# Cross attention, first quarter: each unit's key/value work begins with the chunk that comes from DRAM

## Chip, cores and metric

The kernel is one program on one core of a Trainium2 chip. The metric is device time in microseconds (us). Before the change three runs took 3841.57, 3847.80 and 3852.76 us, a median of 3847.8 us.

## What is computed

Two decoder layers on 16 sequences of 112 rows of width 512 (float32), with a context of 375 rows for each sequence. Layer 0 is causal self attention, a block with fp8-rounded activations (self attention and cross attention, whose results are joined before one projection), and a mixture of experts; layer 1 is self attention, cross attention over the context, and a feed-forward with ternary weights. The change lies in the cross part of the fp8 block, whose mathematics is this:

```
qx  = layernorm(fp8_linear(ln_out, wqx))               # 16 heads of 128
kvx = cond @ w_kv_x.T                                  # cond: 16 x 375 x 512
kx, vx = split(kvx);  kx = layernorm(kx)               # 8 groups of 128 each
xout = softmax(qx @ kx.T / sqrt(128)) @ vx             # two heads share a group
catq = fp8(concat(core, xout) / proj_smooth);  out = catq @ wproj.T * scale
```

## The kernel before, in words

`stage_fp8_cross` (L1178) treats the 16 heads in four quarters `q` of four heads (two key/value groups), and in each quarter the 16 sequences `b`. One pair (q, b) is a **unit**, an object of `CrossUnit` (L1060); there are 64. I number the units of the first quarter 0 to 15.

A unit loads the transposed context `ct` (two buffers) and, where a tile of 128 rows begins, the rounded activations `xq`. Its steps are:

- `queries` (L1093): the projection `ps_q`, eight matmuls, only for 14 of the 16 units of a quarter (14 tiles of 128 rows cover the 16 x 112 rows), then `normed`, into `qn`.
- `keys_values(ch)` (L1102) for the chunks 0, 1 and 2 of 125 context rows: four matmuls of 128x512 in float32 into `ps_kv` (L1113), `normed` into `kn`, and a copy into `vn` (L1118). **In the first quarter chunk 2 has no matmuls here.** Its product was made in the stage before (`EarlyKeys.product`), stored in `kv_dram`, and is loaded behind the first 250 context rows of `ct` (L1077, `self.early`).
- `normed` (L1082) takes three engines: a square on ScalarE (`sq`, L1088), a sum on VectorE (`cu_v`, L1089), reciprocal square root by two instructions on GpSimd (L517, L518), and the product on VectorE (`kn` or `qn`, L1091).
- `transpose` (L1120): `qn` and `kn` through TensorE to `qt` and `kt` (ScalarE copies them out). I call the transposes of the two key groups kT0 and kT1.
- `scores(heads)` (L1134), for heads 0 and 1, then 2 and 3: the product `ps_s`, the row extreme `ex_m` (VectorE, L1056), the exponential `pr` with its row sum (ScalarE, L1057), the reciprocal `cx_s` (L1145) and the scaling of `pr` (L1148), both VectorE.
- `transpose_probs` (L1150): `pr` through TensorE into `ps_pt` (L1156), copied by ScalarE into `pt`; each of the three chunks takes four transposes, one for each head.
- `values` (L1161): `ps_av`, then `smooth_fp8` on VectorE and GpSimd (`r_y`, `r_m`, `r_t`, `r_o`); two units later `output` (L1172), the product `ps_acc` and its addition to `x` on VectorE (L931).

The loop is a pipeline over two units: at step n it projects the new unit n while it scores unit n-1. In program order that is: queries of n, chunk 0 of n, scores 0 and 1 of n-1, chunk 1 of n, scores 2 and 3 of n-1, chunk 2 of n, output of n-2, transposed probabilities and values of n-1, transposes of n.

`kn` has one buffer, so no chunk of a new unit's `kn` can be written before the keys of the unit before it have been transposed. `vn` and `ct` have two. PSUM tags: `mm` (ps_q, ps_kv) three banks, `tr` two, `sc` (ps_s, ps_av) two, `acc` one. From the third unit on, the weights of the next quarter are prepared beside the units (`Weights.step`, L596: loads `raw` and `w_kv`, `w_mean` on VectorE, `w_cross` on ScalarE and GpSimd).

The order in which each engine runs its instructions in this stage isn't that of the program. A scheduler of the framework sorts them, by program order as priority and by its own idea of when an operand is ready; it pulls work forward where it thinks an engine would stand still. Each engine then runs its list strictly in order. SyncE (SP) issues all loads of the stage from one such list.

Of the kernel before, what the change touches and what calls it, by code (L numbers as in the profile page):

```python
# [54 lines left out]
def tile_of(b):  # L55


    return None if b % 8 == 7 else b - b // 8
# [42 lines left out]
def chunks(slot, at, c, n, rows=P):  # L101
    return slot[:rows, at : at + c * n].rearrange("p (c n) -> p c n", c=c)
# [13 lines left out]
def load_pieces(k, what, src, widths):  # L116
    pieces, at = [], 0
    for n in widths:
        pieces.append(load_piece(k, what, src[:, at : at + n]))
        at += n  # L120
    return pieces


def behind(k):


    return k.tc.issue_after(k.last_load.ins)
# [38 lines left out]
class NormedRows:  # L166
# [4 lines left out]
    def __init__(self, k, wk, rows, tags=("tr",)):  # L171
        self.k, self.wk, self.rows, self.tags = k, wk, rows, tags
        self.at = [sum(n for _, _, n in rows[:i]) for i in range(len(rows) + 1)]
        self.xt = wk.tile([P, KC, self.at[-1]], F32, tag="xt", name="xt", bufs=1)
        self.mv, self.rs = row_stats(k, [r for r, _, _ in rows])
        self.xn = []
        for i in range(min(2, len(rows))):
            self.normalize(i)
# [360 lines left out]
class Weights:  # L539
# [30 lines left out]
    def keys_values(self, k, src):  # L570
        with behind(k):
            self.kv = load_piece(k, "kv", src)
        return lambda: self.center_keys(k, self.kv), None
# [486 lines left out]
class CrossUnit:  # L1060
# [3 lines left out]
    def __init__(self, k, wk, q, b, w, heads):  # L1064
        self.k, self.wk, self.q, self.b, self.w = k, wk, q, b, w
        self.heads, self.tile = heads, tile_of(b)
        if self.tile is not None:
            self.xq = wk.tile([P, KC, P], F32R, tag="xq", name="xq", bufs=2)
            k.nc.sync.dma_start(out=self.xq.bitcast(F32), in_=k.xx_dram[self.tile])
        self.ct = ct = wk.tile([P, KC * SC + 12], F32, tag="ct", name="ct", bufs=2)  # L1070
        if q == 0:
            n = SC - CC
            self.ct, self.early = chunks(ct, 0, KC, n), ct[:CC, KC * n :].rearrange(
                "p (h d) -> p h d", d=P
            )
            k.nc.sync.dma_start(out=self.ct, in_=k.a["ctx_t"][b][:, :, :n])
            k.last_load = k.nc.sync.dma_start(out=self.early, in_=k.kv_dram[b])  # L1077
        else:
            self.ct = chunks(ct, 0, KC, SC)
            k.last_load = k.nc.sync.dma_start(out=self.ct, in_=k.a["ctx_t"][b])  # L1080
# [21 lines left out]
    def keys_values(self, ch):  # L1102
        k, wk, nc = self.k, self.wk, self.k.nc
        w = chunks(self.w.kv, 0, KC, 512)
        if ch == 0:
            self.kn = wk.tile([CC, NCH, 2, P], F32, tag="kn", name="kn", bufs=1)
            self.vn = wk.tile([CC, NCH, 2, P], F32, tag="vn", name="vn", bufs=2)
        if ch == NCH - 1 and self.q == 0:
            pkv = self.early
        else:  # L1110
            pkv = k.psum.tile([CC, 4, P], F32, tag="mm", name="ps_kv", bufs=3)
            for c in range(KC):
                nc.tensor.matmul(  # L1113
                    pkv, self.ct[:, c, ch * CC : (ch + 1) * CC], w[:, c, :],
                    start=c == 0, stop=c == KC - 1,
                )
        self.normed(self.kn[:, ch], pkv[:, 0:2, :])
        nc.scalar.copy(self.vn[:, ch], pkv[:, 2:4, :])  # L1118
# [59 lines left out]
def stage_fp8_cross(k):  # L1178


    with k.stage("s2b", mm=3, tr=2, sc=2, acc=1) as wk:
        units = []
        for n in range(4 * B + 2):
            q, b = divmod(n, B)
            new = last = None
            if q < 4:
                if b == 0:
                    w, heads = k.next_w, Heads()
                new = CrossUnit(k, wk, q, b, w, heads)
                units.append(new)  # L1190
                new.queries()
                new.keys_values(0)
            if 0 < n <= 4 * B:
                last = units[n - 1]
                last.scores((0, 1))
            if new:
                new.keys_values(1)
            if last:
                last.scores((2, 3))
            if new:  # L1200
                new.keys_values(2)

            first = new is None or q == 0
            if n > 1 and first:
                units[n - 2].output()
            if last:
                last.transpose_probs()
            if n > 1 and not first:
                units[n - 2].output()
            if last:  # L1210
                last.values()
            if new:
                new.transpose()
            if b == 2 and q < 3:
                k.next_w = Weights(k, "cross", q + 1, wk, raw=2)
            if b >= 2 and q < 3:
                k.next_w.step(1)
            if b == 2 and q == 3:
                with behind(k):
                    k.weights["shared"] = load_pieces(k, "shared", k.a["shared_w"], MOE_WIDTHS)  # L1220
# [565 lines left out]
def stage_ffn(k):  # L1786
# [66 lines left out]

STAGES = (
    stage_attn0, stage_fp8_self, stage_fp8_cross, stage_moe, stage_attn1,
    stage_cross1, stage_ffn,
)
# [147 lines left out]
```

## Time and profile before

| | |
|---|---|
| median of three runs | 3847.8 us |
| profiled execution | 3842.72 us, of which the span from first to last instruction is 3841.0 us |
| granted TensorE clock, mean | 0.975 |
| TensorE busy over the span | 3627.2 us (94%) |
| VectorE, ScalarE, GpSimd busy | 1764.6, 1437.4, 926.1 us |
| first quarter of the cross stage | from about 930 to 1262 us of the span |
| costliest group | L1113, `ps_kv`, 1408 records, 638.3 us |

How to read it: all times in views of the trace are microseconds from the start of the span. A float32 matmul shows as two records. The TensorE records overlap in the trace, since their ends are modelled, so I compare starts with starts. In a timeline, a row has start, length, engine, line, operation and tiles; `[1.36 <-DVE pr L1148]` at its end says that the engine stood idle for 1.36 us before it, until VectorE's instruction of line 1148 released it.

### The profile page before, as it was taken

The page shows a single profiled execution, that of the slowest core. Times are in us where ns is not written, and L with a number is a line of the kernel's source. Part 1 is how long each engine was busy: PE and PEld are TensorE (multiplying, and loading weights), DVE is VectorE, ACT ScalarE, POOL GpSimd, SP SyncE. Part 2 cuts the span into 40 slices and gives each one's busy share as a digit, 9 for nine tenths or more (in the row PEclk, how much of TensorE's full clock was granted, in tenths as well). Part 3 has the DMA queues.
Part 4 walks back from the last instruction along what each step waited for, and adds up shares of the span by engine and source line. Part 5 has one row for each costly group of instructions (what it writes and reads, how often), then busy time and mean ns, then how long its engine had stood idle before and what let it go on. Part 6 is the DMA issues. An engine that isn't in the chain of part 4 may idle for free.

```text
span 3841.0 us, 46297 instructions
## 1 busy us (share of the span) xinstructions
PE 3627.2 (94%) x16482; PEld 2338.3 (61%) x16482; DVE 1764.6 (46%) x3872; ACT 1437.4 (37%) x4149; POOL 926.1 (24%) x1314
## 2 busy tenths in 40 slices
PE   7888898899899999999999999999989999999999
PEld 4455787787555566656666654555544445556788
DVE  4445777776544544544445543111243343214333
ACT  2455675554444444444444430111123341112222
POOL 2333555553322322222222210000132220000000
PEclk8999899999999999999999999999989999999999
DMA  2125333432211211211121113999830022222000
GB/s 78 52 101 172 113 101 120 132 128 79 76 51 52 76 52 46 71 49 52 42 84 49 44 47 121 314 320 317 298 129 12 1 71 82 72 74 81 11 12 17
DMA packets 118117, 364.56 MB, mean 95 GB/s; under 512 B 13280, under 2 KB 33248, under 8 KB 108848
## 3 DMA queue, kind: packets, MB, share of 16 engines
q1 hardware_dynamic: 105504, 332.20, 26.7%
q0 software_dynamic: 5040, 16.52, 1.2%
q10 hardware_dynamic: 7344, 12.89, 0.9%
q8 instruction: 131, 2.15, 0.2%
q14 instruction: 98, 0.80, 0.1%
HBM read 317.09 MB, written 44.47 MB: 94 GB/s over the span
## 4 chain that ended last, share of the span: by engine, by line
PE 69%; DVE 8%; POOL 5%; DMA 3%; issue 2%; ACT 2%; SPq 0%; POOLq 0%; ACTq 0%; DVEq 0%
PE ps_kv L1113 14%; PE ps L1470 5%; PE ps_av L1166 4%; PE ps_s L1141 3%; PE ps_y L1488 3%; PE ps_q L695 3%; PE ps_acc L695 3%; PE ps_u L1832 3%; PE ps_o L350 3%; PE ps_o L1814 3%; PE ps_g L1832 3%; PE ps_q L1583 3%; PE ps_p L1676 3%; PE ps_pt L1156 2%; PE ps_v L1598 1%
## 5 line engine op out<-in xcount | busy, mean ns | idle before, releaser
L1113 PE MATMUL ps_kv<-w_kv,ct 128*125 128x512 f32 x1408 | 638.3, 593 | 0.0
L1113 PEld LDWEIGHTS ps_kv<-w_kv,ct 128*125 128x125 f32 x1408 | 260.5, 188 | 276.1 <-issue 242.0
L536 POOL TENSOR_TENSOR r_o<-r_t,r_m 128x64 fp32r<-128x64 bf16 (+6 forms) x224 | 146.6, 671 | 326.6 <-DVE r_t L534 302.9
L1057 ACT ACTIVATE pr<-ps_s,ex_m 112x375 f32<-112x375 f32 (+1 forms) x272 | 157.4, 579 | 164.6 <-DVE ex_m L1056 154.1
L1089 DVE TENSOR_REDUCE cu_v<-sq 125x2 f32<-125x256 f32 (+1 forms) x248 | 118.6, 478 | 217.5 <-ACT sq L1088 217.5
L1470 PE MATMUL ps<-w_expert,xgt 128*128 128x448 f32 x560 | 216.4, 539 | 0.7 <-ACT xgt L1462 0.7
L517 POOL TENSOR_SCALAR cu_v<-cu_v 125x2 f32<-125x2 f32 (+1 forms) x248 | 48.0, 194 | 635.9 <-DVE cu_v L1089 633.6
L236 POOL TENSOR_TENSOR pr<-pr,nq_s 112x448 f32<-112x448 f32 (+1 forms) x120 | 119.4, 996 | 320.2 <-DVE nq_s L235 266.0
L518 POOL TENSOR_TENSOR cu_v<-cu_v,mhalf 125x2 f32<-125x2 f32 (+1 forms) x248 | 190.0, 766 | 20.4
L231 ACT ACTIVATE pr<-ps_s,nq_m 112x112 f32<-112x112 f32 (+1 forms) x480 | 167.2, 376 | 52.5 <-DVE nq_m L223 48.6
L1141 PE MATMUL ps_s<-kt,qt 128*112 128x375 f32 x512 | 183.5, 479 | 1.7 <-ACT pr L1057 1.3
L1056 DVE TENSOR_REDUCE ex_m<-ps_s 112x1 f32<-112x375 f32 (+1 forms) x272 | 148.2, 545 | 69.1 <-PE ps_s L1703 68.0
L1088 ACT ACTIVATE sq<-ps_kv 125x256 f32<-125x256 f32 x176 | 67.4, 383 | 272.8 <-PE ps_kv L1113 218.5
L511 ACT ACTIVATE qt<-ps_t,turned 128x448 f32<-128x448 f32 (+6 forms) x224 | 116.5, 581 | 130.4 <-PE ps_t L1125 121.8
L1166 PE MATMUL ps_av<-pt,vn 125*128 125x224 f32 x768 | 160.8, 358 | 0.0
L1470 PEld LDWEIGHTS ps<-w_expert,xgt 128*128 128x128 f32 x560 | 103.6, 190 | 92.0 <-issue 91.0
L1156 PEld LDWEIGHTS ps_pt<-ident,pr 112*125 112x125 f32 x768 | 104.5, 190 | 86.3 <-DVE pr L1148 48.8
L1141 PEld LDWEIGHTS ps_s<-kt,qt 128*112 128x112 f32 x512 | 89.9, 177 | 100.8 <-issue 59.1
L245 ACT COPY ptt<-ps_pt 112x448 f32<-112x448 f32 (+1 forms) x120 | 66.8, 565 | 223.0 <-PE ps_pt L243 223.0
L1156 PE MATMUL ps_pt<-ident,pr 112*125 112x112 f32 x768 | 119.8, 285 | 30.9 <-DVE pr L1148 29.0
L1166 PEld LDWEIGHTS ps_av<-pt,vn 125*128 125x128 f32 x768 | 143.5, 192 | 8.7 <-ACT pt L1159 4.6
L511 ACT ACTIVATE kt<-ps_t,vec 128x375 f32<-128x375 f32 (+7 forms) x240 | 131.4, 588 | 26.0 <-PE ps_t L1131 22.0
(294 smaller groups left out, 7377.4 us busy)
## 6 DMA issues: line engine op xcount, KB each, us to landing
w_expert<-in_moe_w SPq DMA_DIRECT2D x105, 896.0 KB
ct<-in_ctx_t SPq DMA_DIRECT2D x64, 750.0 KB
xq<-xq_dram SPq DMA_DIRECT2D x42, 512.0 KB
xq<-xx_dram SPq DMA_DIRECT2D x56, 256.0 KB
raw<-in_self_w SPq DMA_DIRECT2D x48, 256.0 KB
w_sum<-in_ffn_w SPq DMA_DIRECT2D x12, 1024.0 KB
cn<-in_ctx SPq DMA_DIRECT2D x16, 750.0 KB
xv<-xv_dram SPq DMA_DIRECT2D x48, 224.0 KB
```

What stands on the lines that cost most here:

```text
L231: nc.scalar.activation(pr[:, j, :], self.ps[:, j, r * t : (r + 1) * t], AF.Exp, bias=self.mx[r][:, j : j + 1], scale=-1.0, accum_out=sums[ ...
L511: k.nc.scalar.activation(dst, src, AF.Identity, bias=cols[:, 1:2], scale=cols[:, 0:1])
L518: nc.gpsimd.tensor_tensor(dst, dst, bc(k.minus_half[: dst.shape[0]], [dst.shape[0], n]), ALU.pow)
L695: k.nc.tensor.matmul(out, lhs(c), w[i][:, c, :], start=first and c == 0 and i == 0, stop=last and c == n - 1 and i == 1,)
L1056: nc.vector.tensor_reduce(mx, src, AX.X, ALU.min)
L1057: nc.scalar.activation(dst, src, AF.Exp, bias=mx, scale=-1.0, accum_out=sums)
L1113: nc.tensor.matmul(pkv, self.ct[:, c, ch * CC : (ch + 1) * CC], w[:, c, :], start=c == 0, stop=c == KC - 1,)
L1141: nc.tensor.matmul(ps, self.heads.qt[self.b][:, h, :], self.kt[:, h // 2, :], start=True, stop=True)
L1156: nc.tensor.transpose(ps[:, h, :], self.pr[:, h, ch * CC : (ch + 1) * CC], k.ident[:S, :S])
L1166: nc.tensor.matmul(av[:, 2 * g : 2 * g + 2, :], self.vn[:, ch, g, :], self.pt[:, ch, 2 * g : 2 * g + 2, :], start=ch == 0, stop=ch == NCH - 1,
L1470: nc.tensor.matmul(pp, self.xt[:, c, :], w[:, c, :], start=c == 0, stop=c == 3)
L1832: nc.tensor.matmul(pp, w[:, c, cols], xt[:, part, c, :], start=c == 0 and part == 0, stop=c == 3 and part == 1,)
```

## The change

In the first quarter a unit now does chunk 2 (the one from `kv_dram`) first, ahead of the query projection, and then chunks 0 and 1 where they stood: chunk 0 after the queries, chunk 1 between the two halves of the scores. The place after the second half of the scores, where chunk 2 stood, is empty. The tiles `kn` and `vn` are allocated by whichever chunk comes first. The other quarters keep the order 0, 1, 2. No instruction is added or removed.

```diff
@@ CrossUnit.__init__
         self.heads, self.tile = heads, tile_of(b)
+        self.kn = None
@@ CrossUnit.keys_values
-        if ch == 0:
+        if self.kn is None:
             self.kn = wk.tile([CC, NCH, 2, P], F32, tag="kn", name="kn", bufs=1)
             self.vn = wk.tile([CC, NCH, 2, P], F32, tag="vn", name="vn", bufs=2)
@@ stage_fp8_cross
                 units.append(new)
+                steps = [2, 0, 1] if q == 0 else [0, 1, 2]
+                if q == 0:
+                    new.keys_values(steps.pop(0))
                 new.queries()
-                new.keys_values(0)
+                new.keys_values(steps.pop(0))
             if 0 < n <= 4 * B:
                 last = units[n - 1]
                 last.scores((0, 1))
             if new:
-                new.keys_values(1)
+                new.keys_values(steps.pop(0))
             if last:
                 last.scores((2, 3))
-            if new:
-                new.keys_values(2)
+            if new and steps:
+                new.keys_values(steps.pop(0))
```

In the changed file, lines from 1067 on are numbered one higher, and more from the loop on.

## The prediction

> **What bounds the kernel now.** I read the busy table first. TensorE is busy for 94% of the span, so this change can win only TensorE's idle time in the stage it touches. The table by stage comes next: the stretch of the first quarter, then the second, whose units the change leaves alone.
>
> ```profile
> PE 3627.2 (94%) x16482; PEld 2338.3 (61%) x16482; DVE 1764.6 (46%) x3872; ACT 1437.4 (37%) x4149; POOL 926.1 (24%) x1314
> ```
>
> The stretches (length, then PE, PEld, DVE, ACT, POOL busy, granted clock, DMA share, GB/s):
>
> ```profile
> 930.00:1262.00 332.00, 306.95 (x1196) 192.67 (x1197) 167.25 (x416) 150.60 (x366) 92.50 (x169) 0.99 0.22 66
> 1262.00:1598.00 336.00, 331.39 (x1235) 202.56 (x1234) 164.70 (x391) 145.07 (x348) 86.48 (x159) 0.99 0.17 52
> ```
>
> TensorE lacks 25 us in the first quarter and 4.6 in the second. The view of waits for TensorE in the first quarter (total, times, longest) says for whom:
>
> ```profile
> PE ps_pt L1156 <- DVE pr L1148: 22.2, 16, 3.1
> PE ps_acc L695 <- POOL r_o L536: 1.4, 1, 1.4
> PE ps_t L1131 <- DVE kn L1091: 1.3, 2, 0.8
> ```
>
> So 22.2 us go to the transposes of the probabilities, once in a unit, waiting for VectorE's scaling of heads 2 and 3. The timeline lists them: ten of 1.36 to 1.39 (13.7), three of 0.58 to 0.90 (2.1), and 0.48, 2.85 and 3.07 in units 0 and 1. **That is the ceiling.** Why VectorE is late shows in its timeline, beside ScalarE's and TensorE's, for one of the ten:
>
> ```profile
> 1041.65 0.41 DVE L1089 TENSOR_REDUCE cu_v<-sq 125x2 f32<-125x256 f32 x1
> ...
> 1042.24 0.19 ACT L1057 ACTIVATION_READ_ACCUMULATOR pr<-ps_s,ex_m 112x1 f32 x1
> ...
> 1043.15 0.42 DVE L1091 TENSOR_TENSOR kn<-ct,cu_v 125x256 f32<-125x256 f32 x1 [1.09 <-POOL cu_v L518]
> 1043.50 0.16 DVE L1145 RECIPROCAL cx_s<-cx_s 112x2 f32<-112x2 f32 x1
> 1043.57 0.73 DVE L931 SCALAR_TENSOR_TENSOR x<-ps_acc,c_proj,x 128x512 f32<-128x512 f32 x1
> ...
> 1044.22 0.73 DVE L1148 TENSOR_SCALAR pr<-pr,cx_s 112x375 f32<-112x375 f32 x2
> ...
> 1044.68 0.47 PE L1156 MATMUL ps_pt<-ident,pr 112*125 112x112 f32 x2 [1.36 <-DVE pr L1148]
> ```
>
> The row sums are there at 1042.24 + 0.19 = 1042.43. But chunk 2's `kn<-ct` stands at the head of VectorE's list and waits for GpSimd until 1043.15, and then `x` is served first. The chain of waits runs the same way in these units: POOL L518, DVE kn, cx_s, x, pr, PE.
>
> **What moves.** I compared the built order of both programs on every engine. The scheduler doesn't put chunk 2 at the start of a unit. Its square and sum (`sq<-ct`, `cu_v`) keep their slot after the second half of the scores, but now belong to the unit one later. Its `kn<-ct` can't run there (`kn` has one buffer) and lands behind kT1, after `r_t`. So the slot before `cx_s` loses `kn<-ct`, and `x` falls behind `pr`. The scheduler also regroups TensorE: of the query projection only one matmul, not four, stands before head 2's transposes. The other four go between kT0 and kT1, where one matmul of chunk 0 stood; that one goes behind kT1. From the start of the second quarter all lists are the same.
>
> **One of the ten units, step by step**, from the second score pair (1038.67).
> - VectorE: sums at +3.76. `cx_s` follows 0.03 later and `pr` another 0.21 later, as in the first score pair of this unit (1037.68, 1037.71, 1037.92); TensorE starts 0.46 after `pr` (1044.22 to 1044.68). Head 2 is ready at +4.46 instead of +6.01, 1.55 us sooner.
> - TensorE: first four transposes at +3.11 as before, one q matmul at +3.47, ready at +3.79 (0.32 from that q to a transpose, as at 1044.92 to 1045.24). It waits 0.67 for head 2. Head 3 follows 0.33 later (the pair of `pr` takes 0.73, one 0.40), q x3 after 0.14, the last four transposes after 0.79: +5.72. Before, they began at 1046.17, or +7.50. Saved: 1.78.
> - Given back: the four q matmuls. Between kT0 and kT1 they take 1.28 (the second quarter has this order: 1258.78 to 1260.06), as long as the chunk 0 matmul that leaves (1029.75 to 1031.02, 1.27). That one, 0.86 (half of a 1.72 pair, from 2.58 for three), now lies behind kT1. Net 0.92.
> - `ps_av`: ScalarE no longer squares `ps_q` (0.60) between the copies of `pt`; 2.40 as in the unit without a projection (1066.54 to 1068.94), not 2.47. Together 0.99.
>
> Ten units: **9.9 us**. The units with waits of 0.61 and 0.58 have no query; a chunk 0 matmul (0.86) leaves the gap and `pr` comes 1.55 sooner, so both meet at about 1062.95 in the first; less 0.1 for head 3, **1.0** for both. In the one of 0.90 TensorE's order stays, the wait goes: **0.9**.
>
> **Units 0 and 1** need each queue. At the start, chunk 2's `kn` of unit 0 is made while TensorE still projects, so the wait of 0.51 before its transposes goes; the regrouped transposes give 0.6 in all. SP is more important:
>
> ```profile
> 945.50 0.55 SPq L1076 DMA_DIRECT2D ct<-in_ctx_t  x1
> 946.09 0.51 SPq L1077 DMA_DIRECT2D ct<-kv_dram  x1
> 946.65 0.33 SPq L112 DMA_DIRECT2D w_kv<-in_cross_w  x1
> ```
>
> The first waits for the buffer of unit 0's `ct`, held by `kn<-ct` (944.93 + 0.42). Then the last reader is the chunk 1 matmuls (until 941.8), so all three go 3.5 us sooner, and `w_kv` lands near 951.7, not 955.2. That matters, since VectorE's new list has three `w_mean` reductions and a `w_kv` subtraction ahead of unit 0's first `pr`. With `w_kv` at 951.7: `pr` of heads 0 and 1 at 954.4 (0.48 goes), and, adding the list's durations, `pr` of head 2 at 960.6 instead of 962.47: **1.9**. Were `w_kv` still at 955.2, the same sum ends at 963.4, a loss of 0.9; the ceiling is 3.3 + 0.6. I take 1.9, as the release is plain. Unit 1 loses a `kn<-ct` that took 1.48; `cx_s` could go 1.75 sooner, but GpSimd's `w_cross` (1.26 at 982.53) may block `pr` beside it: 0.4 to 1.74, I take **1.2**.
>
> What is costed at nothing: `sq<-ct` needs its load a unit earlier, but that is issued about 5 us sooner, when chunk 1's matmuls free the buffer, some 18 us before the square; cover gone, ScalarE would hold the exponentials. `xq` is issued about 5 us later with 11 left. `x` behind `pr` frees the one `acc` bank 18 us before it is needed. `qn` (679 to 693 ns) with its GpSimd wait now stands ahead of chunk 0's sum and `ex_m` of head 0: I get `qn` done at 1034.85, and chunk 0's square can be summed at 1035.45 (1034.59 + 0.86), so 0.6 to spare.
>
> **A rule against the change.** Row: `kn<-ct` took 424 to 1478 ns; the longest ran beside GpSimd's `w_cross`. The Trainium skill ("SBUF — State Buffer", section "Who interferes with whom") says that a VectorE instruction with two SBUF inputs and a GpSimd instruction that reads SBUF exclude each other for the whole instruction. `kn<-ct` has two such inputs, which that one row bears out, and its new place is beside `r_o` (1.17 for a unit); in the old one GpSimd had just finished. By the median row it costs 0.42; by the rule up to 1.06 more in each unit, 10.6 us over the ten if nothing covered it: gain 4. I find cover: 0.6 as above, and the 0.4 left over delays only head 0, while VectorE is done with the first `pr` pair 0.7 before chunk 1's sum. So 0 on the path, and I keep some of it for the range.
>
> **Sum.** 9.9 + 1.0 + 0.9 + 1.9 + 1.2 = 14.9 us. Against the profiled execution's 3842.7 that is 3827.8; against the median of three runs, 3847.8, it is 3832.9. The profiled execution lies among the lower of the four; I say **3832**.
>
> **Rivals.**
> - *Part of it is lost on VectorE's list* (22%): port blocking, or `pr` slowed by it, costs about 0.7 a unit, gain 7: 3840. For it: 1478 ns above, and a `pr` pair of 1.77 instead of 0.73 beside `w_cross`. Against: both in unit 1 alone.
> - *All waits vanish* (6%): gain 22, 3825. Against it: one q matmul is too little cover, 0.67 stays.
> - *Slower* (4%): `sq<-ct` stands on ScalarE ahead of head 2's exponential. If its load lands after that, heads 2 and 3 slip and TensorE has lost three q matmuls of cover. At the old delay of `pr` a unit is 0.63 longer (0.92 + 0.63 = 1.55, the break-even being 0.92 of lateness), 6.3 for ten: 3854. It decides once a load takes over 19 us. Against: the whole queue of 1.77 MB ending with `w_kv` took 9.7 us.
> - *Nothing moved* is excluded by the built orders.
>
> **Numbers.** The forecast itself has 68%. About 0.3% (11.5 us) is what a measurement tells from no change; 14.9 is close to it and medians of three scatter by 5, so faster 0.70, same 0.26, slower 0.04. Bounds: ten units at 0.6 to 1.4, unit 0 from -0.9 to 3.9, unit 1 from 0.4 to 1.74, so gains from about 7 to 22; with the scatter 3822 to 3843.
>
> **What would show it.** The wait of L1157 for `pr` falls from 22.2 to about 11.6 us (0.7 to 0.8 in the ten, 2.1 and 1.9 in units 0 and 1) with TensorE's busy time unchanged; units of 19.8 become 18.8; `w_kv` issues near 943; `kn<-ct` stands behind `r_t`, some of over 1 us. I am wrong if TensorE waits for `kt` or `ex_m` instead, if `sq<-ct` waits for a DMA, or if the ten waits stay above 1.2.

## The result, and the profile after

The changed kernel took 3834.2 us (median of 16 runs) beside 3848.1 us (16 runs of the kernel before). The ratio is **0.9964, 95% interval 0.9953 to 0.9975**: 0.36% faster, or about 14 us. The interval includes a gain of 0.25%, so "over 0.3%" is likely and not certain. The forecast was 3832, with a range of 3822 to 3843.

The profiled execution has a span of 3823.6 us, 17.4 less than before. Of that, 15.4 us lie in the first quarter. What comes before it ran 2.9 us shorter and what follows it 0.9 us longer, although the change doesn't touch either. The four lines below are from views whose lines of before were shown in the prediction: the busy table, the stretch of the first quarter (length, then PE, PEld, DVE, ACT and POOL busy, clock, DMA share, GB/s) and TensorE's waits in it.

```profile
PE 3617.8 (95%) x16482; PEld 2333.7 (61%) x16482; DVE 1770.9 (46%) x3872; ACT 1439.6 (38%) x4149; POOL 929.7 (24%) x1314
```

```profile
930.00:1245.00 315.00, 303.42 (x1193) 191.65 (x1192) 174.43 (x419) 150.79 (x364) 93.28 (x168) 0.99 0.23 70
```

```profile
PE ps_pt L1157 <- DVE pr L1149: 10.8, 14, 1.4
PE ps_t L1132 <- DVE kn L1092: 0.8, 1, 0.8
```

The two stretches don't hold quite the same work. Counted from the stage's first `ps_q` to the end of unit 15's last `ps_av`, TensorE is busy for 298.4 us (301.5 before), and about 1.7 of these 3.1 us are a spell at half clock less (last section). What shrank is the wait for `pr`: 22.2 to 10.8 us. One of the ten like units shows how. This is the timeline of all engines:

```profile
1033.19 0.19 ACT L1057 ACTIVATION_READ_ACCUMULATOR pr<-ps_s,ex_m 112x1 f32 x1
...
1033.41 0.17 DVE L1146 RECIPROCAL cx_s<-cx_s 112x2 f32<-112x2 f32 x1 [0.41 <-ACT pr L1057]
1033.61 0.74 DVE L1149 TENSOR_SCALAR pr<-pr,cx_s 112x375 f32<-112x375 f32 x2
...
1034.08 0.80 PE L1157 MATMUL ps_pt<-ident,pr 112*125 112x112 f32 x4 [0.54 <-DVE pr L1149]
1034.27 0.75 DVE L931 SCALAR_TENSOR_TENSOR x<-ps_acc,c_proj,x 128x512 f32<-128x512 f32 x1
```

Before, `kn<-ct` (with 1.09 of idle time ahead of it) and `x` stood between the row sum and `pr`. Now `cx_s` waits for ScalarE's row sum and for nothing else, and `x` comes after `pr`. TensorE waits 0.54 where it waited 1.36, and these units take 18.93 us instead of 19.81.

### The profile page after: what moved, and what is told of

The parts are those of the page before. It is cut to its first block, busy times and chain, and to the rows that moved or that the text cites. A ratio compares the mean times of both kernels' runs of the same rounds, so it can differ in the third digit from the quotient of the medians.

```text
span 3823.6 us, 46289 instructions
## 1 busy us (share of the span) xinstructions
PE 3617.8 (95%) x16482; PEld 2333.7 (61%) x16482; DVE 1770.9 (46%) x3872; ACT 1439.6 (38%) x4149; POOL 929.7 (24%) x1314
## 5 line engine op out<-in xcount | busy, mean ns | idle before, releaser
L914 DVE TENSOR_TENSOR r_y<-ps_av,r_smooth 128x448 bf16<-128x448 f32 x128 | 79.2, 619 | 126.8 <-PE ps_av L1167 122.8
```

## How the experiments are read

Whole executions scatter by several us, but the first quarter repeats to 0.3 us: a second profile of the changed kernel gave 309.75 us after 310.01. So each run is read by its first quarter, from the stage's first `ps_q` to the end of unit 15's last `ps_av`. The first four expectations count to the start of that `ps_av`, which is 2.4 us less (323.0 before, 307.6 after). "Half clock" counts the windows of 3.41 us in the quarter in which TensorE's granted clock was 0.50 (last section); each costs up to 1.7 us, half its length, and all of them lie in units 0 to 2. All numbers of the table are from the traces, except the ratio, which is to the kernel before on the same chip, with its 95% interval.

| kernel | `w_kv` issued after | wait for `pr` | half clock | units 0-2 | units 3-15 | quarter | ratio |
|---|---|---|---|---|---|---|---|
| before | 13.58 | 22.2 | 2 | 76.60 | 248.83 | 325.43 | 1 |
| changed | 10.12 | 10.8 | 1 | 70.42 | 239.59 | 310.01 | 0.9964 (0.9953-0.9975) |
| 1 before, `kn<-ct` on GpSimd | 13.71 | 10.4 | 3 | 75.18 | 239.55 | 314.73 | 0.9969 (0.9951-0.9988) |
| 2 changed, keys in place | 13.38 | 21.1 | 3 | 75.22 | 248.29 | 323.51 | 0.9999 (0.9984-1.0014) |
| 3 before, `x` later | 13.58 | 21.9 | 3 | 75.95 | 248.88 | 324.83 | 0.9992 (0.9976-1.0008) |
| 4 order 0, DRAM, 1 | 10.12 | 15.3 | 0 | 70.10 | 248.94 | 319.04 | 0.9978 (0.9969-0.9988) |
| 7 mixed order | 10.13 | 8.4 | 0 | 67.99 | 239.60 | 307.59 | 0.9948 (0.9932-0.9963) |
| 9 changed, one subtraction on VectorE | 10.12 | 8.1 | 0 | 65.59 | 239.57 | 305.16 | 0.9939 (0.9922-0.9955) |
| 10 before, the same | 13.58 | 20.4 | 1 | 72.12 | 248.83 | 320.95 | 0.9970 (0.9955-0.9986) |

In this table units 3 to 15 take one of two lengths, 239.6 or 248.3 to 248.9; runs 1 to 4 show what decides. Where TensorE's matmuls of q are regrouped (changed, 1, 4, 7, 9), 0.9 us of what units 0-2 gain is only work that moves behind `ps_av` and comes back in unit 15.

## Experiments on the steady units

Four theories of where the gain comes from: A, the place of `kn<-ct` in VectorE's list; B, earlier loads and the clock in units 0 and 1; C, that a unit begins with the chunk; D, that `x` comes after `pr`.

**1. Before, with the DRAM chunk's product on GpSimd.**

```diff
-        nc.vector.tensor_tensor(dst, src, bc(var.unsqueeze(2), [t, n, P]), ALU.mult)
+        eng = nc.gpsimd if pool else nc.vector        # pool: src is the DRAM chunk
+        eng.tensor_tensor(dst, src, bc(var.unsqueeze(2), [t, n, P]), ALU.mult)
```

> The kernel before, its order of chunks untouched; only the multiplication that normalises the DRAM chunk (kn<-ct) is given to GpSimd, so that it cannot stand in VectorE's list ahead of cx_s. Theory A (the gain is that slot: kn<-ct no longer between the scores' row sums and the normalisation of the probabilities): TensorE's wait for pr in the first quarter falls from 22.2 to 10-13 us, the quarter (first ps_q of the stage to unit 15's last ps_av) from 323.0 to 307-311 us, the total by 12-16 us to 3832-3836. Theory B (the gain comes from the earlier release of ct and so from earlier loads, and from the clock in units 0 and 1): the loads are not earlier here, so at most 3 us, quarter 320-323. Theory C (a unit must begin with the chunk): no gain, quarter 322-324.

Measured: wait 10.4, quarter 312.3 by the count of the expectation, median 3835.6. TensorE's wait for `pr` in the quarter:

```profile
PE ps_pt L1158 <- DVE pr L1150: 10.4, 13, 2.1
```

Theory A holds for the steady units: with the chunk still last, and `w_kv` no earlier, units 3 to 15 are as short as in the changed kernel (239.55 and 239.59). As in the changed kernel, `x` falls behind `pr` here; run 3 shows what that alone is worth. The quarter misses A's band by 1.3 us, and the miss lies in units 0 to 2, which gain 1.4 us where those of the changed kernel gain 6.2. Theory C falls.

**2. Changed, with the normalised keys written over the loaded ones.**

```diff
-        self.normed(self.kn[:, ch], pkv[:, 0:2, :])
+        self.normed(self.early[:, 0:2, :] if pkv is self.early else self.kn[:, ch], pkv[:, 0:2, :])
```

The transposes read them from there.

> The changed kernel, a unit still begins with the DRAM chunk, but its normalised keys are written over the loaded ones in ct, not into kn. So the multiplication waits neither for kn nor for anything of the unit before it, and the built order has it ahead of cx_s again, with the matmuls of q grouped as before (4, 1, 3). Theory A (the slot ahead of cx_s): the gain is gone though the chunk comes first; wait for pr 20-23 us, quarter 320-324, total within 3 us of before. Theory C (beginning with the chunk is what pays, whatever VectorE's list): quarter 306-311, total 12-16 us under before. Theory B (earlier loads): ct is held longer here, so no gain either, and w_kv lands as late as before or later: together with the first run it parts A from B.

Measured: wait 21.1, quarter 321.1 by that count, ratio 0.9999. VectorE's timeline in one of its units:

```profile
1043.34 0.42 DVE L1093 TENSOR_TENSOR ct<-ct,cu_v 125x256 f32<-125x256 f32 x1 [1.09 <-POOL cu_v L518]
1043.68 0.15 DVE L1148 RECIPROCAL cx_s<-cx_s 112x2 f32<-112x2 f32 x1
1043.76 0.73 DVE L931 SCALAR_TENSOR_TENSOR x<-ps_acc,c_proj,x 128x512 f32<-128x512 f32 x1
```

A unit begins with the DRAM chunk and nothing is gained. The product, `ct<-ct` here, is back ahead of `cx_s` with the same 1.09 of idle time, and `x` with it. In the changed kernel it is the single buffer of `kn` that keeps it out of this place.

**3. Before, with the output projection behind the transposed probabilities.**

```diff
-            first = new is None or q == 0
+            first = new is None
```

> The kernel before, but the output projection of the first quarter is put behind the transposes of the probabilities in the program, which takes VectorE's x additions behind pr; kn<-ct stays ahead of cx_s. Theory A (kn<-ct ahead of cx_s): most of the loss stays; wait for pr 15-21 us, quarter 315-323, total 0-8 us under before. Theory D (it is the x additions' place behind pr alone that pays): wait for pr 10-13 us, quarter 307-311, total 12-16 us under before.

Measured: wait 21.9, quarter 322.4, ratio 0.9992. The built order has `x` behind `pr`, as in the changed kernel, and such a unit takes 19.65 instead of 19.81. So `x` alone is worth about 0.16 us in such a unit; over units 3 to 15 nothing is left of it (248.88 beside 248.83). Theory D falls. The idle time ahead of `kn<-ct` is the same 1.09.

**4. Changed, in the order 0, DRAM, 1.**

```diff
-                steps = [2, 0, 1] if q == 0 else [0, 1, 2]
-                if q == 0:
-                    new.keys_values(steps.pop(0))
+                steps = [0, 2, 1] if q == 0 else [0, 1, 2]
                 new.queries()
                 new.keys_values(steps.pop(0))
+                if q == 0:
+                    new.keys_values(steps.pop(0))
```

> The changed kernel with the chunks of a first-quarter unit in the order 0, DRAM, 1 instead of DRAM, 0, 1. In the built order kn<-ct and its row sum stand after chunk 0's and before the scores' maxima; the slot ahead of cx_s is empty as in the changed kernel and TensorE's list is the same. Theory A (only that the slot ahead of cx_s is empty): as the changed kernel, wait for pr 10-12.5 us, quarter 306.5-309.5, total within 3 us of 3834. Theory C (it must be the unit's first chunk): some of the gain is lost, quarter 312-320. If the multiplication (0.42-0.9 us) delays chunk 0's keys or the maxima: 0.4-0.9 us a unit more, quarter 313-320, shown as a wait of TensorE for kn or of ScalarE for ex_m.

Measured: wait 15.3, quarter 316.6. Theory A as I had put it fails here. The slot ahead of the second `cx_s` is empty, yet a unit takes 19.71. The third case of the expectation came true (theory C's band holds 316.6 too, but runs 1 and 2 speak against C). VectorE and ScalarE in one unit:

```profile
1029.54 0.39 ACT L1089 ACTIVATE sq<-ps_kv 125x256 f32<-125x256 f32 x1 [2.53 <-PE ps_kv L1114]
...
1032.42 0.42 DVE L1092 TENSOR_TENSOR kn<-ct,cu_v 125x256 f32<-125x256 f32 x1 [0.52 <-POOL cu_v L518]
1032.76 1.00 DVE L1056 TENSOR_REDUCE ex_m<-ps_s 112x1 f32<-112x375 f32 x2
...
1034.79 0.74 DVE L1149 TENSOR_SCALAR pr<-pr,cx_s 112x375 f32<-112x375 f32 x2
...
1035.77 0.54 DVE L1056 TENSOR_REDUCE ex_m<-ps_s 112x1 f32<-112x375 f32 x1
...
1039.23 0.79 PE L1157 MATMUL ps_pt<-ident,pr 112*125 112x112 f32 x4 [1.15 <-DVE pr L1149]
```

Here two products and their GpSimd waits stand ahead of the maxima of heads 0 and 1. The first maximum starts 3.22 us after chunk 0's square (in the changed kernel 0.75: 1025.11 to 1025.86). The first `pr` pair then falls just ahead of head 2's maximum, which comes 6.23 after that square instead of 5.51 (1025.11 to 1030.62). These 0.72 us make up most of the longer unit (19.71 against 18.93). So the sentence of theory A has to be wider: **what pays is that `kn<-ct`, with its wait for GpSimd, stands nowhere between a unit's scores and its `pr`.**

## Experiments on units 0 to 2

Runs 1 and 4 also part the first three units. Run 4 has the early `w_kv` (10.12 us after the stage's start) and loses in all later units; its units 0 to 2 take 70.10 us. Run 1 has the late `w_kv` and the free slot: 75.18. Without the 0.9 us of moved work these are gains of 5.6 and 0.5 us. So about 5 of the 15.4 us come from the first three units (6.2 less 0.9), and they go with the earlier load.

Part of this is the clock. Run 4 has no window at half clock and run 1 has three, worth up to 5.1 us, as much as these two runs differ; the changed kernel has one less than the kernel before. So the two runs show the load together with the clock that follows a long wait, not the load alone. The wait that the load causes is seen directly. VectorE's timeline, before and changed, where `w_kv` is first read:

```profile
955.25 0.42 DVE L613 TENSOR_REDUCE w_mean<-w_kv 128x2 f32<-128x256 f32 x1 [2.25 <-DMA w_kv<-in_cross_w]
955.59 0.15 DVE L1145 RECIPROCAL cx_s<-cx_s 112x2 f32<-112x2 f32 x1
```

```profile
949.30 0.74 DVE L613 TENSOR_REDUCE w_mean<-w_kv 128x2 f32<-128x256 f32 x2
949.96 0.16 DVE L616 TENSOR_SCALAR w_mean<-w_mean 128x2 f32<-128x2 f32 x1
```

Before, VectorE stood still for 2.25 us until `w_kv` came, with unit 0's `cx_s` behind it. In the changed kernel it finds `w_kv` there.

**5 and 6. The weight preparation begun two units later, in both kernels.**

```diff
-            if b == 2 and q < 3:
+            if b == 4 and q < 3:
...
-            if b >= 2 and q < 3:
+            if b >= 4 and q < 3:
```

> The kernel before, with the preparation of the next quarter's weights begun two units later (units 2 and 3 instead of 0 and 1). It parts what units 0 and 1 lose to the late w_kv load and to VectorE's and GpSimd's weight work from what they lose to kn<-ct ahead of cx_s. Before, unit 0's ps_av ends 36.0 us and unit 1's 57.8 us after the stage's first ps_q. Theory B (the late load and the weight work made units 0 and 1 slow): 31.5-33.5 and 51-53.5 us, waits for pr of about 1.4 there as in the ten, and no fall of the granted clock; the loss then comes back in units 2 to 4, total within 5 us of before. Rival (units 0 and 1 are slow because of the slot): over 35 and over 56 us.

> The changed kernel with the same delay of the weight preparation. In the changed kernel unit 0's ps_av ends at 31.0 and unit 1's at 53.7 us, after waits for pr of 1.09, 1.38, 1.33 and 0.97. If the weight work beside the first units is what the change could not shorten there: 30-31 and 49-50.5 us, waits of about 0.5, no fall of the clock, and the waits come in units 2 to 4 instead. If the first units are slow for another reason: 53 us or more. Total within 5 us of the changed kernel.

Measured: unit 0's `ps_av` ends at 31.66 us and unit 1's at 49.23 in the kernel before (36.02 and 57.75 with the preparation beside them), and at 29.90 and 46.46 in the changed kernel (30.99 and 53.71). Theory B holds: the weight work with its load made these units slow, in both kernels. The two move together here, so these runs don't part the one from the other. Unit 1 ended earlier than both expectations had it, and the waits in units 0 and 1 were shorter too: 0.91 and 0.90 in the kernel before, none in the changed kernel. The loss only moves to units 2 and 3, where TensorE then waited 2.86 and 4.81 for `pr` in the one and 2.93 and 1.85 in the other. The quarters end 2.2 and 1.6 us later than without the delay (327.64 and 311.57); ratios 1.0001 (0.9987 to 1.0014) and 0.9953 (0.9927 to 0.9978).

**7. The order 0, DRAM, 1 in the first two units only.**

```diff
-                steps = [2, 0, 1] if q == 0 else [0, 1, 2]
-                if q == 0:
+                steps = ([2, 0, 1] if b > 1 else [0, 2, 1]) if q == 0 else [0, 1, 2]
+                if q == 0 and b > 1:
                     new.keys_values(steps.pop(0))
                 new.queries()
                 new.keys_values(steps.pop(0))
+                if q == 0 and b < 2:
+                    new.keys_values(steps.pop(0))
```

> The changed kernel, but the first two units take the order 0, DRAM, 1, the others DRAM, 0, 1. With 0, DRAM, 1 throughout unit 1 had no such loss (its period was 19.05 us instead of 22.14), while each later unit was 0.8 us longer. Expected: units 0 and 1 as there (ps_av ends near 32.7 and 51.2 us), later periods of 18.9 us, the quarter 2-4 us shorter than in the changed kernel (to unit 15's last ps_av 306-308 us instead of 310.0), total 0-4 us under it. If the loss in unit 1 belongs to the weight work and only its place moves, it turns up in unit 2 and the quarter stays within 1 us of 310.

Measured: unit 0 ends at 32.32, unit 1 at 51.19, the quarter at 307.59: 2.4 us shorter than the changed kernel, as expected. Up to 1.7 us of it is the window at half clock that is missing here. Once more, beside the changed kernel on one chip:

> The changed kernel with the order 0, DRAM, 1 in the first two units only, once more and beside the changed kernel on the same chip. Its profiled quarter was 2.4 us shorter than the changed kernel's. If that carries to the total: 0.05-0.1% under the changed kernel, about 16-20 us under before, ratio to before 0.995-0.996.

> The changed kernel itself, on the same chip as the two other runs of this call. Ratio to before 0.996 as at first, quarter to unit 15's ps_av 310.0 us, waits for pr 10.8 us, and the waits of the first units again 1.09, 1.38, 1.33, 0.97 and 1.21 us.

The quarter repeats (307.58 against 309.75; the changed kernel's first waits 1.09, 1.28, 1.33, 0.97, 1.21). The totals, 0.9954 (0.9935 to 0.9973) and 0.9966 (0.9949 to 0.9982), are not told apart by these intervals.

**8. Chunk 1 behind the second half of the scores.**

```diff
-            if new:
+            if new and q:
                 new.keys_values(steps.pop(0))
```

> The changed kernel with chunk 1 moved behind the second half of the scores, into the place that chunk 2 left. Then VectorE has no kn<-ps_kv between the two row maxima of a half, and TensorE has more matmuls between scores and transposes. If what is left of the wait (0.53 us a unit) goes: quarter to unit 15's ps_av 302-306 us instead of 310.0, total 4-8 us under the changed kernel. If TensorE's second half of the scores waits instead for the score banks (ScalarE's pr) since no chunk stands between them: each unit 0.5-2 us longer, quarter 315-335 us.

TensorE's waits in the quarter:

```profile
PE ps_pt L1157 <- ACT pt L1160: 3.9, 10, 0.4
PE ps_s L1142 <- ACT pr L1057: 3.5, 2, 2.9
PE ps_pt L1157 <- DVE pr L1149: 1.2, 2, 1.0
```

The wait for `pr` is all but gone (10.8 to 1.2 us), and the quarter is no shorter: 310.41 us, units of 18.92. Neither of the two expected cases came. Ten waits of 0.39 for ScalarE's copy `pt` have come instead, and the first units wait 2.9 for a score bank. So this move doesn't win the remaining 0.54 us a unit. Why the rest of it doesn't show I haven't followed. The total, 0.9950 (0.9937 to 0.9964), is not told apart from the changed kernel's.

**9. Changed, with one subtraction of the weight preparation on VectorE.** Unit 1 of the changed kernel waits 1.38, 1.33 and 0.97 us for `pr`, more than the 3.07 before. VectorE and GpSimd there:

```profile
969.88 1.27 POOL L641 TENSOR_TENSOR w_cross<-raw,w_cross 128x512 fp32r<-128x512 f32 x1 [2.30 <-ACT w_cross L640]
969.92 1.76 DVE L1149 TENSOR_SCALAR pr<-pr,cx_s 112x375 f32<-112x375 f32 x2
...
975.92 1.75 DVE L1149 TENSOR_SCALAR pr<-pr,cx_s 112x375 f32<-112x375 f32 x2
976.01 1.45 POOL L641 TENSOR_TENSOR w_cross<-raw,w_cross 128x512 fp32r<-128x512 f32 x1
```

Both `pr` pairs took 1.75 us or more beside a `w_cross` of GpSimd, 1.0 more than elsewhere (0.74).

```diff
-                nc.gpsimd.tensor_tensor(lo, raw, hi.bitcast(F32), ALU.subtract)
+                eng = nc.vector if k.lo_vector else nc.gpsimd     # lo_vector: in this stage
+                eng.tensor_tensor(lo, raw, hi.bitcast(F32), ALU.subtract)
```

> The changed kernel, with one subtraction of the weight preparation (the low part of w_cross) moved from GpSimd to VectorE, so that GpSimd reads SBUF for less time beside unit 1. In the changed kernel both pr pairs of unit 1 took 1.76 us beside GpSimd's w_cross instead of 0.73, and unit 1's waits for pr were 1.38, 1.33 and 0.97 us. If the two engines shutting each other out is what failed the forecast for unit 1: pr pairs of 0.73-0.8, waits in unit 1 together 1-2.5 us instead of 3.68, unit 1's ps_av ends near 51.5-52.7 us after the stage's start instead of 53.7. If it is the length of VectorE's own list: no better, 53.7-56 us, since the subtraction lengthens that list.

VectorE in unit 1, now with `w_cross` on its own list:

```profile
970.29 0.74 DVE L1152 TENSOR_SCALAR pr<-pr,cx_s 112x375 f32<-112x375 f32 x2
970.95 0.68 DVE L644 TENSOR_TENSOR w_cross<-raw,w_cross 128x512 fp32r<-128x512 f32 x1
...
975.63 0.75 DVE L1152 TENSOR_SCALAR pr<-pr,cx_s 112x375 f32<-112x375 f32 x2
```

Both pairs are back at 0.74 and 0.75, unit 1's waits fall from 3.68 to 1.10, and its `ps_av` ends at 49.25 us instead of 53.71. That is better than expected, and more than the waits: the window at half clock is gone too. Unit 0 pays a little (a wait of 1.67 instead of 1.09, its end at 31.58 instead of 31.00). The same subtraction takes 0.68 us on VectorE and 1.27 to 1.45 on GpSimd. Total: 3821.8 us, ratio 0.9939 (0.9922 to 0.9955), where the changed kernel on the same chip had 0.9966: the lowest ratio of all kernels run here, though its interval overlaps those of runs 6, 7 and 8. In the first quarter it is 4.9 us faster than the changed kernel. By the end of the stage's 64th unit the two profiles of that chip differ by 11.3 us (1325.89 and 1314.63), so the quarters whose weights are prepared the same way gain too.

**10. The same in the kernel before.**

> The kernel before, with the same subtraction of the weight preparation moved from GpSimd to VectorE. On the changed kernel this move took 4.9 us off the first quarter (310.0 to 305.2 to the end of unit 15's ps_av) and 14 us off the total. If the two gains have different causes (the slot ahead of cx_s in units 2 to 15; GpSimd and VectorE shutting each other out in the weight work of units 0 and 1 and in the other quarters) they add: the slot's waits of 1.36 stay in the ten units, unit 1 no longer waits 3.07, the quarter is 318-322 us instead of 325.4, the total 8-15 us under before. If the changed kernel's gain was mostly that it kept the two engines apart, this run reaches it: quarter 308-313 us, total 20 us or more under before, waits of about 0.5 in the ten units.

Measured: quarter 320.95 (4.5 us shorter), the ten waits still 1.36 to 1.45, ratio 0.9970 (0.9955 to 0.9986). Units 3 to 15 take 248.83, exactly as before. The two gains add: 15.4 + 4.5 = 19.9, and with both it is 20.3 us. About 1.3 of the 4.5 us is luck: unit 0 waits 2.85 as before, but no window at half clock follows (last section), and its `ps_av` takes 2.57 us instead of 3.91. That the causes differ rests on units 3 to 15, where nothing moved.

## Why the prediction was right, and where it was off

- **The sum: right, and in part by luck.** The quarter lost 15.4 us where 14.9 was forecast. Units 2 to 15 gave 0.9 less than forecast and units 0 and 1 gave 1.4 more, and the two misses cancel. The clock, for which the prediction had no term, gave 1.35 of it, in unit 0's `ps_av`.
- **The ceiling and the slot: right.** The wait for `pr` fell to 10.8 us (11.6 forecast), and runs 1, 2 and 4 show the cause that the prediction gave, in the wider wording of run 4.
- **The ten units: 0.88 instead of 0.99 us each.** Head 2 is ready 4.48 us after the second score pair (4.46 forecast), and the one q matmul stands at 3.47 as put. The term that was off is the one from there to the last four transposes: heads 2 and 3 and q take 1.35 (1034.08 to 1035.43), not 1.26, so 1.67 is saved, not 1.78. Units 2 to 15 save 10.96 by the starts of `ps_av`, where 9.9 + 1.0 + 0.9 = 11.8 was forecast.
- **Work that only moves.** In that count unit 2 saves 1.63 and unit 15 loses 0.87. Four q matmuls that stood ahead of `ps_av` now stand behind it, one unit later; unit 15 gets them back. The prediction's sum took them as given back in each unit, which comes to the same in the total.
- **Units 0 and 1: 4.5 instead of 3.1 us together, for reasons partly other than forecast.** The step "`w_kv` 3.5 us sooner" was right (3.46 by the stage's start). Unit 0 gained 3.68 by the start of its `ps_av`, not 1.9. The sum over VectorE's list was 1.5 us too long: head 2's `pr` came 26.04 us after the stage's start (956.22 - 930.18), where the forecast's 960.6 means 27.5. I had added row lengths; from start to start a `w_mean` or `w_kv` row of 0.41 takes 0.32 to 0.34 in these timelines. From the first `w_mean` (949.30) to that `pr` the rows and the one wait add up to 8.35 us, and took 6.92.
- **Unit 1: the step that failed.** It was to gain 1.2. By `ps_av` starts it gained 0.79, but 1.35 came from unit 0, whose `ps_av` ran faster (last section), so its own part is a loss of about 0.6, outside the forecast's 0.4 to 1.74. The prediction named GpSimd's `w_cross` beside `pr`, for the pair of heads 2 and 3 only, and took it as a bound. It decided, on both pairs (the pair of heads 0 and 1 took 1.77 before as well, but TensorE did not wait for it then), and run 9 shows it.
- **The rule on VectorE and GpSimd.** `kn<-ct` at its new place took 418 to 1545 ns with a median of 743, where the median had been 425 (shortest, median and longest, in ns):

```profile
L1092 DVE TENSOR_TENSOR kn<-ct,cu_v x16: 418/743/1545, 932.5 to 1206.0; 125x256 f32<-125x256 f32 x16
```

  In 11 of the 16 units a GpSimd `r_o` or `w_cross` ran beside it, and it took 623 ns or more; in the other five none did, and it took 425 or less. So the rule of the Trainium skill ("SBUF — State Buffer", section "Who interferes with whom") applied as feared: 0.2 to 1.1 us in a unit. It was costed at 0 on the path, and that held: in the unit looked at, VectorE waits 0.35 for chunk 0's square after `qn` (0.6 forecast). What GpSimd did cost was at `pr`, in unit 1.
- **The rivals.** The load of `ct` was never late, no transfer held `sq<-ct`, and the waits of the ten units didn't vanish. The first rival (part of the gain lost on VectorE's list) had a mechanism that was there, in unit 1 alone.

## What to carry to other kernels

Read an in-order list by what stands between an operand being ready and its use: a cheap instruction (0.42 us) that itself waits for a third engine (1.09 us) costs every instruction queued behind it. The program order alone did not move it off; a single buffer held it back in the new order, and the same order with that buffer bypassed gained nothing. And when two engines can shut each other out, ask what shares the time with the instruction on the path: here moving 0.68 us of work onto the busier engine made it faster.

## What the runs showed of the hardware

**The clock after a wait.** In the traces TensorE's granted clock falls to one half for a window of 3.41 us, sometimes two, and within one execution all the falls lie on a fixed grid of such windows. Here are windows on that grid (length, PE busy, clock, DMA share, GB/s). Before, with unit 0's wait of 2.85 us, which ends at 962.93:

```profile
957.90:961.31 3.41, 2.19 (x8) 1.00 0.01 2
961.31:964.73 3.42, 1.80 (x8) 1.00 0.26 62
964.73:968.14 3.41, 3.41 (x12) 0.50 0.71 234
```

Run 10, with the same wait of 2.85 us, ending at 961.90, and a later one of 1.70, ending at 980.28:

```profile
957.03:960.44 3.41, 2.02 (x7) 1.00 0.01 2
960.44:963.85 3.41, 1.95 (x10) 1.00 0.32 79
963.85:967.26 3.41, 3.41 (x23) 1.00 0.64 219
...
977.51:980.92 3.41, 1.71 (x8) 1.00 0.29 82
980.92:984.34 3.42, 3.42 (x11) 0.50 0.70 208
```

Changed, with unit 1's waits of 1.33 and 0.97 us:

```profile
974.64:978.05 3.41, 1.10 (x5) 1.00 0.57 187
978.05:981.47 3.42, 3.42 (x11) 0.50 0.46 153
```

Before, 1.62 us of idle time fall into one window, and the next has half the clock. In run 10 the wait is as long, but the grid cuts it into 1.39 and 1.46, and the clock stays; the wait of 1.70 lies within one window, and the clock falls. In the changed kernel two short waits fall into one window, 2.31 us idle, and it falls too. The first quarters of all 14 profiles agree: 16 windows at full clock were followed by half clock, and they had 1.62 to 3.35 us idle; the 1248 others had at most 1.67. So what counts here is not the length of a wait but whether about half of a fixed window is idle, and where the grid lies against the units differs from one execution to the next. (Over whole executions the border is less sharp, between 1.2 and 2.0 us.) The Trainium skill ("TensorE: Matmul & The Clock Gate", Part 1) puts the throttled state after an idle window of about 3.4 us; here about half of that was enough.

A long wait can thus cost more than itself: before, unit 0's `ps_av` took 3.91 us instead of the 2.56 of the changed kernel, whose unit 0 waits 1.09 and keeps its clock.

**GpSimd and VectorE.** A `pr` pair of 0.74 us took 1.76 beside one GpSimd subtraction of 1.27, and stood at 0.74 again once that had gone (run 9). In the kernel before, over all four quarters, the five single `pr` instructions that ran beside such a subtraction took 1.41 to 1.45 us, and the 251 others at most 0.42.
